# Pairing the last key tiles of a cross attention, with its bias as a column and its low parts stored for reuse

## The chip, the core and the metric

The kernel runs on one core of a Trainium2 chip. Its time is the device time of one launch in microseconds; three runs are given, with their median. Profile and trace come from one more execution of the same program.

The engines are named as in the profile: PE is TensorE (matmuls; PEld its weight loads), DVE is VectorE, ACT is ScalarE, POOL is GpSimd, SP is SyncE, from whose queue all DMAs of this kernel are issued. SBUF is the on-chip memory, PSUM the banks that matmuls write to.

## What is computed

The inputs are x (8 batches of 64 tokens, 512 wide) and a context of 8 x 1601 rows, 512 wide. Three blocks are added to x in turn: an attention block with a self attention and a cross attention (16 heads of size 128 in 8 groups), a small attention that keeps the six highest-scored partners of each token, and a feed-forward block with ternary weights. The change lies in the cross attention:

```python
kvx = jnp.einsum('bsi,oi->bso', cond, w_kv_x)
kx, vx = jnp.split(kvx, 2, axis=-1)
kx = _ln(kx.reshape(b, sc, g, d), kxln_w, kxln_b)
vx = vx.reshape(b, sc, g, d)
xout = _gqa(qx, kx, vx).reshape(b, s, nh * d)
```

Here cond is the context (sc = 1601 rows), _ln normalises each key over its 128 elements, multiplies by kxln_w and adds kxln_b, and _gqa is softmax(q k^T / sqrt(d)) v.

## The kernel before

The 1601 context rows of a batch are cut into 13 tiles (TT): twelve of 128 rows and a last one of 65. The eight key groups are worked on in two halves of four (HG = 4), so that the work is a list of 16 items: for each half, the eight batches. Each item has 13 tiles, which makes 208 steps of the main loop, numbered g; 20 more drain it. fp32 accuracy is kept by splitting an operand into a high part, rounded to the fp32r type, and a low part, the rest; a product is then three matmuls (high x high, high x low, low x high).

In each step of the main loop, by lines of the profile:

- **keys(tt)**, L529 to L553: SP loads a tile of the turned context (cTr, L533). ACT rounds it to cThi (L536), POOL subtracts to get cTlo (L537). Twelve matmuls (L542), three products over four blocks of 128 inputs, make the keys of four groups at once, 512 columns, in a PSUM bank. ACT squares them (sq, L547) and copies them (kn, L548). DVE sums the squares (kxv, L549), POOL adds EPS (L550) and takes the power -0.5 (rqk, L173), DVE multiplies (kn, L552). The mean is taken out beforehand, in the weights.
- **keys_t(tt)**, a step later, L555 to L568: four transposes (L219) bring the keys into columns. ACT multiplies by the norm's weight and adds its bias (kthi, L565); DVE makes the rest (kf, L567); ACT adds the bias to that as well (ktlo, L568). Two tiles, at the end of an item three, fill one chunk; an item has six chunks (CHUNKS).
- **scores(ci)**, L570 to L592: matmuls of queries with a chunk's keys (L587); a DVE operation copies the scores from PSUM to S and keeps their maximum (cmx, L591). In the last chunk 321 columns are filled up to 322 with a zero (L575 to L577).
- **maxima**, **exps**: the maximum over the chunks, negated (L596), is the bias of the exponential on ACT (L601).
- LAG = 17 steps later, **context**, **probs_t** and **weigh** (L636 to L678): rows of the context are loaded and split (cr, chi, clo), the exponentials are transposed (L613) and split (phi, plo), and twelve matmuls add probabilities x context to four PSUM banks (L676 to L678). In the first half the context's low part is stored to DRAM (clod<-clo, L658), in the second it is loaded from there (L655, by the helper at L130).
- **values**, **cat**: at the end of an item the sums are multiplied by the value weights.

All other work, the projections of x, self attention, the output projections, the small attention and the preparation of the ternary weights, stands in generators that are pumped a few steps in each round of the main loop (L1225 to L1229): PACE gives the number per round, its second value from round LATER = 142 on. The feed-forward block comes at the end.

Buffers come from pools with fixed numbers: three raw (shared by cTr, cr and other loads), two cThi, two cTlo, three kn, two kf. The kernel is built with a scheduler that puts each engine's instructions in order by priority, following the order of the program and the hints high_priority and issue_after; on the chip each engine and SP's queue then run strictly in that order, waiting for semaphores.

Of the kernel before, what the change touches and what calls it, by code (L numbers as in the profile page):

```python
# [11 lines left out]
F32 = mybir.dt.float32  # L12
F32R = mybir.dt.float32r
# [24 lines left out]
NCH = len(CHUNKS)  # L38
CHUNK_OF = {tt: ci for ci, ch in enumerate(CHUNKS) for tt in ch}
LAG = 17  # L40
ALL = 10 ** 6
# [1 line left out]
SPLIT = 1  # L43
FFN_AT = 6
FAR = 3
PACE = 1.55, 4
LATER = 142
TERNARY_PACE, TERNARY_AT = 0.4, 8
HELD = "held"

# [7 lines left out]
def tile_perceiver(ctx: ExitStack, tc: tile.TileContext, t: dict):  # L58
    nc = tc.nc
    V, A, GP, PE = nc.vector, nc.scalar, nc.gpsimd, nc.tensor  # L60
# [68 lines left out]
    def load(dst, src):  # L129
        nc.sync.dma_start(dst, src)  # L130
        return dst
# [4 lines left out]
    def v3(ap, g):  # L136
        return ap.rearrange("p (g k) -> p g k", g=g)
# [4 lines left out]
    class Late:  # L142
# [13 lines left out]
        ps = staticmethod(lambda tag="b": kxp())  # L156
# [79 lines left out]
    o = 0  # L236
# [24 lines left out]
    def dtile(shape, dt, tag):  # L261
        return dram.tile(shape, dt, tag=tag, name=tag)
# [7 lines left out]
    simd = [dtile([P, S], F32, f"simd{j}") for j in range(NJ - 1)]  # L270

    wpd = [dtile([P, 2, H], F32, f"wpd{c}") for c in range(32)]
    clod = [dtile([SC, H], F32, f"clod{b}") for b in range(NB)]

    codd = [dtile([3, H], F32, f"codd{b}") for b in range(NB)]
# [215 lines left out]
    def key_weights(half):  # L491
# [10 lines left out]
            (V if half else GP).tensor_tensor(lo[:, ic, :], raw, hi[:, ic, :].bitcast(F32), ALU.subtract)  # L502
        return hi, lo

    paced = [None]
    pin = [None]

    class Cross:


        def __init__(self, b, half):
            self.b, self.half = b, half
            self.raw = None
            self.S = {}
            self.kt = {}
            self.kn = {}
            self.pp = {}
# [11 lines left out]
        def keys(self, tt):  # L529

            t0, n = TT[tt]
            raw = mp.tile([P, NIC, P], F32, tag="raw", name=nm("cTr"), bufs=3)
            paced[0] = nc.sync.dma_start(raw[:, :, :n], t["ctxT"][self.b].rearrange("(c p) k -> p c k", p=P)[:, :, t0:t0 + n])  # L533
            chi = mp.tile([P, NIC, P], F32R, tag="cThi", name=nm("cThi"), bufs=2)
            clo = mp.tile([P, NIC, P], F32R, tag="cTlo", name=nm("cTlo"), bufs=2)
            A.copy(chi[:, :, :n], raw[:, :, :n])  # L536
            GP.tensor_tensor(clo[:, :, :n], raw[:, :, :n], chi[:, :, :n].bitcast(F32), ALU.subtract)  # L537
            ps = kxp()
            k = 0
            for st, mv in ((chi, self.wk[0]), (chi, self.wk[1]), (clo, self.wk[0])):  # L540
                for ic in range(NIC):
                    PE.matmul(ps[:n], lhsT=st[:, ic, :n], rhs=mv[:, ic, :], start=k == 0, stop=k == 11)  # L542
                    k += 1
            kn = mp.tile([P, 512], F32, tag="kn", name=nm("kn"), bufs=3)
            sq = mp.tile([P, 512], F32, tag="sq", name=nm("sq"), bufs=1)
            v = sm("kxv", HG)
            A.activation(sq[:n], ps[:n], AF.Square, scale=1.0 / math.sqrt(D))  # L547
            A.copy(kn[:n], ps[:n])  # L548
            V.tensor_reduce(v[:n], v3(sq[:n], HG), AX.X, ALU.add)  # L549
            GP.tensor_scalar(v[:n], v[:n], EPS, None, ALU.add)  # L550
            r = rsqrt(v[:n], n, HG, "rqk")
            pin[0] = V.tensor_tensor(v3(kn[:n], HG), v3(kn[:n], HG), r.unsqueeze(2).to_broadcast([n, HG, D]), ALU.mult)  # L552
            self.kn[tt] = kn  # L553

        def keys_t(self, tt):  # L555

            t0, n = TT[tt]
            ci = CHUNK_OF[tt]
            c0 = TT[CHUNKS[ci][0]][0]
            if ci not in self.kt:  # L560
                self.kt[ci] = [mp.tile([P, HG, KTW], F32R, tag="kt" + x, name=nm("kt" + x), bufs=2) for x in ("hi", "lo")]
            hi, lo = self.kt[ci]
            pt = transpose4(self.kn.pop(tt), n, kxp())
            o = slice(t0 - c0, t0 - c0 + n)
            A.activation(hi[:, :, o], v3(pt, HG)[:, :, :n], AF.Identity, bias=hb["kx"], scale=hw["kx"])  # L565
            kf = mp.tile([P, HG, P], F32, tag="kf", name=nm("kf"), bufs=2)
            V.scalar_tensor_tensor(kf[:, :, :n], v3(pt, HG)[:, :, :n], hw["kx"], hi[:, :, o].bitcast(F32), ALU.mult, ALU.subtract)  # L567
            A.activation(lo[:, :, o], kf[:, :, :n], AF.Identity, bias=hb["kx"])  # L568

        def scores(self, ci):  # L570
            chunk = CHUNKS[ci]
            cw = sum(TT[tt][1] for tt in chunk)
            hi, lo = self.kt.pop(ci)
            N = cw + (cw & 1)
            if N > cw:  # L575
                GP.memset(hi[:, :, cw:N].bitcast(F32), 0.0)
                GP.memset(lo[:, :, cw:N].bitcast(F32), 0.0)  # L577
            sc = mp.tile([P, HG, KTW], F32, tag="S", name=nm("S"), bufs=7)
            self.S[ci] = sc
            per = 512 // N  # L580
            for g0 in range(0, HG, per):
                bank = mainp("s")
                gs = range(g0, g0 + per)

                for k, (a, x) in enumerate(((self.qhi, hi), (self.qlo, hi), (self.qhi, lo))):
                    for i, g in enumerate(gs):
                        PE.matmul(bank[:, i * N:(i + 1) * N], lhsT=a[:, g * P:(g + 1) * P], rhs=x[:, g, :N],  # L587
                                  start=k == 0 and i == 0, stop=k == 2, skip_group_check=True)
                for i, g in enumerate(gs):
                    ps = bank[:, i * N:(i + 1) * N]  # L590
                    V.tensor_tensor_reduce(sc[:, g, :cw], ps[:, :cw], zeros.to_broadcast([P, cw]), 1.0, -3.0e38,  # L591
                                           ALU.add, ALU.max, self.mx[:, g * NCH + ci:g * NCH + ci + 1])  # L592

        def maxima(self):
            self.nmx = sm("cnm", HG)
            V.tensor_reduce(self.nmx, v3(self.mx, HG), AX.X, ALU.max, negate=True)  # L596

        def exps(self, ci, g0=0, g1=HG):
            cw = sum(TT[tt][1] for tt in CHUNKS[ci])
# [367 lines left out]
            xs.append((xr, j * P, i * P, P))  # L967
        return z, xs

    def gp_copy(dst, src):  # L970
        GP.tensor_scalar(dst, src, 1.0, 1.0, ALU.mult, ALU.mult)  # L971

    WIDEN = gp_copy, A.copy

    def ffn_weights(f, kind):
# [151 lines left out]
            token_norm(j)  # L1127
            yield

    NT = len(TT)  # L1130
    work = [Cross(b, half) for half in range(2) for b in range(NB)]
    NA = NT * len(work)
    rest = range(1, NJ)
# [3 lines left out]
    bgB = Stream()  # L1137
# [4 lines left out]
    for g in range(NA + LAG + 3):  # L1142
# [26 lines left out]
            work[nA].keys(kA)  # L1169
        if g == 0:  # L1170
            bgA.pump(ALL)
        if g == 2:
            bgA.add(norms(rest), projection("qx", range(4), rest), projection("qx", range(4, 8), range(NJ)),
                    projection("q", range(8), range(NJ)), projection("k", range(4), range(NJ)), projection("v", range(4), range(NJ)))
            bgA.add(*[self_attn(j) for j in range(NJ)])
            bgA.add(attn_consts())
# [132 lines left out]
```

## Time and profile before

| | us |
|---|---|
| median of three runs | 2000.94 |
| lowest, highest | 1998.29, 2001.81 |
| profiled execution | 1998.47 |
| its span, first to last instruction | 1996.7 |
| ACT busy | 1345.9 |
| POOL busy | 682.7 |
| mean granted TensorE clock, of full | 0.987 |

The groups that the change touches, from the page's list of the costliest (line, engine, operation, written and read tiles, shapes, count, then busy us and mean ns of one, then the idle time of its engine before it and what ended it):

```profile
L537 POOL TENSOR_TENSOR cTlo<-cTr,cThi 128x512 fp32r<-128x512 f32 (+1 forms) x208 | 271.1, 1303 | 840.7 <-PE kx L542 443.8
L549 DVE TENSOR_REDUCE kxv<-sq 128x4 f32<-128x512 f32 (+1 forms) x208 | 141.9, 682 | 228.0 <-ACT sq L547 227.7
L567 DVE SCALAR_TENSOR_TENSOR kf<-kx,cols,kthi 128x512 f32<-128x512 f32 (+1 forms) x208 | 151.1, 726 | 60.0 <-ACT kthi L565 58.8
L568 ACT ACTIVATE ktlo<-kf,cols 128x512 fp32r<-128x512 f32 (+1 forms) x208 | 147.4, 709 | 29.0 <-DVE kf L567 28.5
```

Idle time of an engine that isn't the bound costs nothing. In the lines of slices each digit is a fortieth of the span, in tenths of busy time, and 9 is 90% or more. The durations of matmuls overlap: what a matmul takes of PE is read from start to start.

### The profile page before, as it was taken

Reading aid. Unit: us, or ns where it says so; the run is one execution under the profiler, and the core shown is the slowest. Engines: PE = TensorE matmul, PEld = TensorE weight load, DVE = VectorE, ACT = ScalarE, POOL = GpSimd, SP = SyncE. Lnnn points to the kernel's source line nnn. Section 1 sums busy time; section 2 is a strip of 40 time slices with the busy share of each in tenths; the row PEclk is TensorE's granted clock in tenths of the full one; section 3 lists DMA queues with packets and bytes.
Section 4 is the critical chain, followed back from the end, with each engine's and each line's share of the span. In section 5 each row is a group of like instructions: output and inputs, shape, how many; then the busy total and the mean of one; then the engine's idle time right before and its main releaser. Section 6 shows DMA issues by size and latency. Waiting matters only on the chain. (4 is left out here: it accounts for less than half of the span.)

```text
span 1996.7 us, 32526 instructions
## 1 busy us (share of the span) xinstructions
PE 1931.5 (97%) x10709; PEld 1594.1 (80%) x10709; DVE 1357.9 (68%) x3324; ACT 1345.9 (67%) x2932; POOL 682.7 (34%) x807
## 2 busy tenths in 40 slices
PE   6899999999999999999999999999999999999998
PEld 5688887888888888888888888888877777886776
DVE  6868678667778677766775765666577665665665
ACT  6777777677778667765765655665786676676554
POOL 5443434333334434323233323323333323320132
PEclk9999999999999999999999999999999999999989
DMA  6354445466455654556886667656744633564415
GB/s 195 112 151 148 148 146 153 132 193 213 152 150 172 194 179 140 173 180 224 282 268 192 214 225 264 203 185 214 258 133 154 212 110 97 165 205 139 149 56 172
DMA packets 296507, 352.05 MB, mean 176 GB/s; under 512 B 30337, under 2 KB 191233, under 8 KB 296337
## 3 DMA queue, kind: packets, MB, share of 16 engines
q1 hardware_dynamic: 296336, 349.97, 55.8%
q8 instruction: 84, 1.38, 0.3%
q14 instruction: 87, 0.70, 0.1%
HBM read 283.94 MB, written 65.68 MB: 175 GB/s over the span
## 5 line engine op out<-in xcount | busy, mean ns | idle before, releaser
L537 POOL TENSOR_TENSOR cTlo<-cTr,cThi 128x512 fp32r<-128x512 f32 (+1 forms) x208 | 271.1, 1303 | 840.7 <-PE kx L542 443.8
L677 PE MATMUL acc<-plo,chi 128*128 128x512 f32 x768 | 311.7, 406 | 1.0 <-DVE plo L624 1.0
L678 PE MATMUL acc<-phi,clo 128*128 128x512 f32 x768 | 303.4, 396 | 0.0
L549 DVE TENSOR_REDUCE kxv<-sq 128x4 f32<-128x512 f32 (+1 forms) x208 | 141.9, 682 | 228.0 <-ACT sq L547 227.7
L542 PE MATMUL kx<-wkhi,cThi 128*128 128x512 f32 (+1 forms) x832 | 244.3, 415 | 6.6 <-DVE cmx L591 2.5
L676 PE MATMUL acc<-phi,chi 128*128 128x512 f32 x768 | 237.8, 403 | 4.6 <-ACT chi L653 3.4
L565 ACT ACTIVATE kthi<-kx,cols 128x512 fp32r<-128x512 f32 (+1 forms) x208 | 159.5, 767 | 106.8 <-PE kx L219 105.1
L542 PE MATMUL kx<-wklo,cThi 128*128 128x512 f32 (+1 forms) x832 | 231.0, 398 | 0.0
L542 PE MATMUL kx<-wkhi,cTlo 128*128 128x512 f32 (+1 forms) x832 | 226.3, 393 | 0.0
L173 POOL TENSOR_TENSOR rqk<-kxv,mhalf 128x4 f32<-128x4 f32 (+1 forms) x208 | 219.9, 1057 | 16.6
L653 ACT CAST chi<-cr 128x512 fp32r<-128x512 f32 x192 | 118.9, 619 | 137.7 <-PE acc L677 126.2
L536 ACT CAST cThi<-cTr 128x512 fp32r<-128x512 f32 (+1 forms) x208 | 125.6, 605 | 120.0 <-PE kx L542 48.4
L601 ACT ACTIVATE S<-S,cnm 128x256 f32<-128x256 f32 (+1 forms) x384 | 196.8, 520 | 1.5 <-DVE cnm L596 1.5
L567 DVE SCALAR_TENSOR_TENSOR kf<-kx,cols,kthi 128x512 f32<-128x512 f32 (+1 forms) x208 | 151.1, 726 | 60.0 <-ACT kthi L565 58.8
L542 PEld LDWEIGHTS kx<-wklo,cThi 128*128 128x128 f32 (+1 forms) x832 | 156.2, 188 | 39.7
L542 PEld LDWEIGHTS kx<-wkhi,cTlo 128*128 128x128 f32 (+1 forms) x832 | 153.5, 185 | 39.3 <-issue 0.8
L552 DVE TENSOR_TENSOR kn<-kn,rqk 128x512 f32<-128x512 f32 (+1 forms) x208 | 144.7, 695 | 57.0 <-POOL rqk L173 55.5
L542 PEld LDWEIGHTS kx<-wkhi,cThi 128*128 128x128 f32 (+1 forms) x832 | 147.2, 189 | 40.8 <-DVE cmx L591 5.0
L591 DVE CUSTOM_DVE_ANT_0 S<-s,zeros 128x256 f32<-128x256 f32 (+1 forms) x384 | 149.7, 429 | 43.8 <-PE s L587 43.5
L568 ACT ACTIVATE ktlo<-kf,cols 128x512 fp32r<-128x512 f32 (+1 forms) x208 | 147.4, 709 | 29.0 <-DVE kf L567 28.5
L676 PEld LDWEIGHTS acc<-phi,chi 128*128 128x128 f32 x768 | 139.0, 189 | 34.9 <-ACT chi L653 4.6
L677 PEld LDWEIGHTS acc<-plo,chi 128*128 128x128 f32 x768 | 145.2, 189 | 25.7 <-DVE plo L624 1.5
(339 smaller groups left out, 3938.3 us busy)
## 6 DMA issues: line engine op xcount, KB each, us to landing
cTr<-in_ctxT SPq DMA_DIRECT2D x192, 256.0 KB
cr<-in_ctx SPq DMA_DIRECT2D x192, 256.0 KB
ws<-wpd SPq DMA_DIRECT2D x88, 512.0 KB
clod<-clo SPq DMA_DIRECT2D x96, 256.0 KB
clo<-clod SPq DMA_DIRECT2D x96, 256.0 KB
wv<-in_wkv SPq DMA_DIRECT2D x64, 256.0 KB
tern<-in_ffn_w SPq DMA_DIRECT2D x64, 256.0 KB
wpd<-ws SPq DMA_DIRECT2D x32, 512.0 KB
```

Source lines behind the costliest of these rows:

```text
L173: GP.tensor_tensor(y[:n], v, mhalf[:n, :k], ALU.pow)
L537: GP.tensor_tensor(clo[:, :, :n], raw[:, :, :n], chi[:, :, :n].bitcast(F32), ALU.subtract)
L542: PE.matmul(ps[:n], lhsT=st[:, ic, :n], rhs=mv[:, ic, :], start=k == 0, stop=k == 11)
L552: pin[0] = V.tensor_tensor(v3(kn[:n], HG), v3(kn[:n], HG), r.unsqueeze(2).to_broadcast([n, HG, D]), ALU.mult)
L565: A.activation(hi[:, :, o], v3(pt, HG)[:, :, :n], AF.Identity, bias=hb["kx"], scale=hw["kx"])
L567: V.scalar_tensor_tensor(kf[:, :, :n], v3(pt, HG)[:, :, :n], hw["kx"], hi[:, :, o].bitcast(F32), ALU.mult, ALU.subtract)
L568: A.activation(lo[:, :, o], kf[:, :, :n], AF.Identity, bias=hb["kx"])
L591: V.tensor_tensor_reduce(sc[:, g, :cw], ps[:, :cw], zeros.to_broadcast([P, cw]), 1.0, -3.0e38, ALU.add, ALU.max, self.mx[:, g * NCH + ci:g ...
L601: A.activation(self.S[ci][:, g, :cw], self.S[ci][:, g, :cw], AF.Exp, bias=self.nmx[:, g:g + 1], accum_out=self.su[:, g * NCH + ci:g * NCH ...
L676: PE.matmul(self.U[ic], lhsT=chi[:n, s], rhs=phi[:n], start=tt == 0, stop=False)
L677: PE.matmul(self.U[ic], lhsT=chi[:n, s], rhs=plo[:n], start=False, stop=False)
L678: PE.matmul(self.U[ic], lhsT=clo[:n, s], rhs=phi[:n], start=False, stop=False)
```

## The change

- **Pairing.** In 14 of the 16 items (all but batches 0 and 1 of the first half) the last tile holds 64 rows of each of two neighbouring batches, 128 in all; its keys are computed once, in the even batch's round, and the odd batch's round computes none. The 65th row of all eight batches is computed in odd_keys, once per half (rounds 30 and 110), and copied to its place by ACT.
- **Bias as a column.** The norm's bias is no longer added to the keys. It gives each row of scores one and the same addend, q times bias, which the softmax takes out again. It stands as column 322 of the last chunk; its score is copied from PSUM (cqb) and enters the maximum. So L568 goes, and the operation of L567 writes ktlo itself.
- **The norm's constant** is column 129 of the squares (ksq), written once; L550 goes.
- **The turned context's low parts** of the twelve full tiles are stored to DRAM in the first half (clotd) and loaded in the second in place of L537.
- PACE and LATER change, background steps are scheduled at a lower priority, and the scratch for dynamic DMA is cut to 1024 bytes.

```diff
+UNPAIRED = 2
+ODD_AT = 30, 110
-PACE = 1.55, 4
-LATER = 142
+PACE = 1.64, 4
+LATER = 140
...
+    def normed_keys(wk, chi, clo, n, held=False):
+        ps = kxp()
+        k = 0
+        for st, mv in ((chi, wk[0]), (chi, wk[1]), (clo, wk[0])):
+            for ic in range(NIC):
+                PE.matmul(ps[:n], lhsT=st[:, ic, :n], rhs=mv[:, ic, :], start=k == 0, stop=k == 11)
+                k += 1
+        kn = mp.tile([P, 512], F32, tag="kn2" if held else "kn", name=nm("kn"), bufs=1 if held else 3)
+        sq = ksq
+        v = sm("kxv", HG)
+        A.activation(sq[:n, :, :D], v3(ps[:n], HG), AF.Square, scale=1.0 / math.sqrt(D))
+        A.copy(kn[:n], ps[:n])
+        V.tensor_reduce(v[:n], sq[:n], AX.X, ALU.add)
+        r = rsqrt(v[:n], n, HG, "rqk")
+        pin[0] = V.tensor_tensor(v3(kn[:n], HG), v3(kn[:n], HG), r.unsqueeze(2).to_broadcast([n, HG, D]), ALU.mult)
+        return kn
+    def turned(kn, n, parts, r0=0):
+        hi, lo = parts
+        pt = kxp()
+        for g in range(HG):
+            PE.transpose(pt[:, g * P:g * P + n], kn[:, g * P:(g + 1) * P], ident[r0:r0 + n, r0:r0 + n])
+        src = v3(pt, HG)[:, :, :n]
+        A.activation(hi, src, AF.Copy, scale=hw["kx"])
+        V.scalar_tensor_tensor(lo, src, hw["kx"], hi.bitcast(F32), ALU.mult, ALU.subtract)
+    def odd_keys(half):
...
+        kn = normed_keys(wk[half], chi, clo, NB)
...
+        turned(kn[:NB], NB, [x[:, :, :, 0] for x in oddk[half]])
...
+    GP.memset(ksq[:, :, D:], EPS)
...
         def keys(self, tt):
             t0, n = TT[tt]
+            pair = tt == NT - 1 and self.paired
+            if pair and self.b % 2:
+                return
...
+            for bi in range(2 if pair else 1):
+                w = S if pair else n
+                paced[0] = nc.sync.dma_start(raw[:, :, bi * S:bi * S + w], t["ctxT"][self.b + bi].rearrange("(c p) k -> p c k", p=P)[:, :, t0:t0 + w])
...
             A.copy(chi[:, :, :n], raw[:, :, :n])
-            GP.tensor_tensor(clo[:, :, :n], raw[:, :, :n], chi[:, :, :n].bitcast(F32), ALU.subtract)
...
-            GP.tensor_scalar(v[:n], v[:n], EPS, None, ALU.add)
...
+            if self.half and tt < NT - 1:
+                load(clo.bitcast(F32), clotd[self.b][tt])
+            else:
+                GP.tensor_tensor(clo[:, :, :n], raw[:, :, :n], chi[:, :, :n].bitcast(F32), ALU.subtract)
+                if tt < NT - 1:
+                    nc.sync.dma_start(clotd[self.b][tt], clo.bitcast(F32))
+            self.kn[tt] = normed_keys(self.wk, chi, clo, n, pair)
...
         def keys_t(self, tt):
...
-            A.activation(hi[:, :, o], v3(pt, HG)[:, :, :n], AF.Identity, bias=hb["kx"], scale=hw["kx"])
-            kf = mp.tile([P, HG, P], F32, tag="kf", name=nm("kf"), bufs=2)
-            V.scalar_tensor_tensor(kf[:, :, :n], v3(pt, HG)[:, :, :n], hw["kx"], hi[:, :, o].bitcast(F32), ALU.mult, ALU.subtract)
-            A.activation(lo[:, :, o], kf[:, :, :n], AF.Identity, bias=hb["kx"])
...
+            r = self.b % 2 * S
+            turned(kn[r:r + S], S, [x[:, :, o:o + S] for x in self.kt[ci]], r)
+            for x, y in zip(self.kt[ci], oddk[self.half]):
+                A.copy(x[:, :, o + S:o + S + 2], y[:, :, self.b, :])
...
         def scores(self, ci):
...
+                    if N > cw:
+                        V.tensor_copy(self.qb[:, g:g + 1], ps[:, cw:N])
         def maxima(self):
+            top = sm("ctop", HG)
+            V.tensor_reduce(top, v3(self.mx, HG), AX.X, ALU.max)
+            V.tensor_tensor(top, top, self.qb, ALU.add)
             self.nmx = sm("cnm", HG)
-            V.tensor_reduce(self.nmx, v3(self.mx, HG), AX.X, ALU.max, negate=True)
+            V.tensor_tensor(self.nmx, self.qb, top, ALU.subtract)
...
+        if g in ODD_AT:
+            odd_keys(work[nA].half)
...
-            with tc.issue_after(pin[0].ins), tc.issue_after(paced[0].ins) if bg is bgB else nullcontext():
+            with tc.issue_after(pin[0].ins), tc.issue_after(paced[0].ins) if bg is bgB else nullcontext(), tc.high_priority( -100):
                 bg.pump(n)
...
-    nc = _bacc.Bacc("TRN2", target_bir_lowering=False, num_devices=1)
+    nc = _bacc.Bacc("TRN2", target_bir_lowering=False, num_devices=1, dynamic_dma_scratch_size=1024)
```

More of the change, by code (lines that the diff above doesn't have):

```diff
@@ L38 @@
 NCH = len(CHUNKS)
+NT = len(TT)
+ODD_AT = 30, 110
+UNPAIRED = 2
 CHUNK_OF = {tt: ci for ci, ch in enumerate(CHUNKS) for tt in ch}
@@ L272, in tile_perceiver @@
     wpd = [dtile([P, 2, H], F32, f"wpd{c}") for c in range(32)]
+    clotd = [[dram.tile([P, NIC, P], F32, name=f"clotd{b}_{k}") for k in range(len(TT) - 1)] for b in range(NB)]
     clod = [dtile([SC, H], F32, f"clod{b}") for b in range(NB)]
@@ new lines, in turned @@
+    def turned(kn, n, parts, r0=0):
[6 more added lines that the diff above has]
+        V.scalar_tensor_tensor(lo, src, hw["kx"], hi.bitcast(F32), ALU.mult, ALU.subtract)
+    oddk = {}
+    def odd_keys(half):
+        raw = load(mp.tile([P, 512], F32, tag="raw", name=nm("oc"), bufs=3)[:NB], t["ctx"][:, SC - 1, :])
+        pt = kxp()
+        for ic in range(NIC):
+            PE.transpose(pt[:, ic * NB:(ic + 1) * NB], raw[:, ic * P:(ic + 1) * P], ident[:NB, :NB])
+        chi = mp.tile([P, NIC, P], F32R, tag="cThi", name=nm("cThi"), bufs=2)
+        clo = mp.tile([P, NIC, P], F32R, tag="cTlo", name=nm("cTlo"), bufs=2)
+        src = v3(pt[:, :NIC * NB], NIC)
+        A.copy(chi[:, :, :NB], src)
+        V.tensor_tensor(clo[:, :, :NB], src, chi[:, :, :NB].bitcast(F32), ALU.subtract)
+        kn = normed_keys(wk[half], chi, clo, NB)
+        oddk[half] = [const.tile([P, HG, NB, 2], F32R, tag=f"odd{x}", name=nm("odd")) for x in ("h", "l")]
+        for x, y in zip(oddk[half], kb2):
+            gp_copy(x[:, :, :, 1], y.bitcast(F32).unsqueeze(2).to_broadcast([P, HG, NB]))
+        turned(kn[:NB], NB, [x[:, :, :, 0] for x in oddk[half]])
@@ L505, in tile_perceiver, with gp_copy @@
+    def gp_copy(dst, src):
+        GP.tensor_scalar(dst, src, 1.0, 1.0, ALU.mult, ALU.mult)
+    kb = ctile([P, HG], F32, "kb")
+    kb2 = ctile([P, HG], F32R, "kbhi"), ctile([P, HG], F32R, "kblo")
+    V.tensor_copy(kb, hb["kx"].to_broadcast([P, HG]))
+    V.tensor_copy(kb2[0], kb)
+    V.tensor_tensor(kb2[1], kb, kb2[0].bitcast(F32), ALU.subtract)
+    ksq = ctile([P, HG, D + 1], F32, "ksq")
+    GP.memset(ksq[:, :, D:], EPS)
     paced = [None]
@@ L513, in __init__ @@
             self.raw = None
+            self.paired = half > 0 or b >= UNPAIRED
             self.S = {}
@@ L516, in __init__ @@
             self.kn = {}
+            self.qb = sm("cqb", HG, bufs=2)
             self.pp = {}
@@ L531, in keys @@
             t0, n = TT[tt]
+            pair = tt == NT - 1 and self.paired
+            if pair and self.b % 2:
+                return
             raw = mp.tile([P, NIC, P], F32, tag="raw", name=nm("cTr"), bufs=3)
-            paced[0] = nc.sync.dma_start(raw[:, :, :n], t["ctxT"][self.b].rearrange("(c p) k -> p c k", p=P)[:, :, t0:t0 + n])
+            if pair:
+                n = P
+            for bi in range(2 if pair else 1):
+                w = S if pair else n
+                paced[0] = nc.sync.dma_start(raw[:, :, bi * S:bi * S + w], t["ctxT"][self.b + bi].rearrange("(c p) k -> p c k", p=P)[:, :, t0:t0 + w])
             chi = mp.tile([P, NIC, P], F32R, tag="cThi", name=nm("cThi"), bufs=2)
@@ L536, in keys @@
             A.copy(chi[:, :, :n], raw[:, :, :n])
-            GP.tensor_tensor(clo[:, :, :n], raw[:, :, :n], chi[:, :, :n].bitcast(F32), ALU.subtract)
[L538 to L549, printed above, removed]
-            GP.tensor_scalar(v[:n], v[:n], EPS, None, ALU.add)
-            r = rsqrt(v[:n], n, HG, "rqk")
-            pin[0] = V.tensor_tensor(v3(kn[:n], HG), v3(kn[:n], HG), r.unsqueeze(2).to_broadcast([n, HG, D]), ALU.mult)
-            self.kn[tt] = kn
+            if self.half and tt < NT - 1:
[5 more added lines that the diff above has]
+            self.kn[tt] = normed_keys(self.wk, chi, clo, n, pair)
+            if pair:
+                work[self.half * NB + self.b + 1].kn[tt] = self.kn[tt]
         def keys_t(self, tt):
@@ L561, in keys_t @@
                 self.kt[ci] = [mp.tile([P, HG, KTW], F32R, tag="kt" + x, name=nm("kt" + x), bufs=2) for x in ("hi", "lo")]
-            hi, lo = self.kt[ci]
-            pt = transpose4(self.kn.pop(tt), n, kxp())
-            o = slice(t0 - c0, t0 - c0 + n)
-            A.activation(hi[:, :, o], v3(pt, HG)[:, :, :n], AF.Identity, bias=hb["kx"], scale=hw["kx"])
-            kf = mp.tile([P, HG, P], F32, tag="kf", name=nm("kf"), bufs=2)
-            V.scalar_tensor_tensor(kf[:, :, :n], v3(pt, HG)[:, :, :n], hw["kx"], hi[:, :, o].bitcast(F32), ALU.mult, ALU.subtract)
-            A.activation(lo[:, :, o], kf[:, :, :n], AF.Identity, bias=hb["kx"])
+            o = t0 - c0
+            kn = self.kn.pop(tt)
+            if tt < NT - 1 or not self.paired:
+                turned(kn[:n], n, [x[:, :, o:o + n] for x in self.kt[ci]])
+                if n & 1:
+                    for x, y in zip(self.kt[ci], kb2):
+                        gp_copy(x[:, :, o + n:o + n + 1], y.bitcast(F32).unsqueeze(2))
+                return
+            r = self.b % 2 * S
+            turned(kn[r:r + S], S, [x[:, :, o:o + S] for x in self.kt[ci]], r)
+            for x, y in zip(self.kt[ci], oddk[self.half]):
+                A.copy(x[:, :, o + S:o + S + 2], y[:, :, self.b, :])
         def scores(self, ci):
@@ L574, in scores @@
             N = cw + (cw & 1)
-            if N > cw:
-                GP.memset(hi[:, :, cw:N].bitcast(F32), 0.0)
-                GP.memset(lo[:, :, cw:N].bitcast(F32), 0.0)
             sc = mp.tile([P, HG, KTW], F32, tag="S", name=nm("S"), bufs=7)
@@ L968, in ffn_rows @@
         return z, xs
-    def gp_copy(dst, src):
-        GP.tensor_scalar(dst, src, 1.0, 1.0, ALU.mult, ALU.mult)
     WIDEN = gp_copy, A.copy
@@ L1128, in norms @@
             yield
-    NT = len(TT)
     work = [Cross(b, half) for half in range(2) for b in range(NB)]
```

## The prediction

> **What bounds the kernel now.** I read the page's busy table first, then the slices, then the waits of PE, then the timeline of PE for the price of one tile.
>
> ```profile
> PE 1931.5 (97%) x10709; PEld 1594.1 (80%) x10709; DVE 1357.9 (68%) x3324; ACT 1345.9 (67%) x2932; POOL 682.7 (34%) x807
> PE   6899999999999999999999999999999999999998
> PEclk9999999999999999999999999999999999999989
> DMA  6354445466455654556886667656744633564415
> ```
>
> PE is busy for 97% of the span and in the highest tenth in all but a few slices at both ends; the next engines, DVE and ACT, stand at 68% and 67%. The granted clock is full in nearly every slice, so the span is PE's work plus its gaps. A busy PE need not be dense, as the ends of matmuls are modelled, so the second view is what PE waits for from 100 to 1800 us (engine, line, releaser: total, times, longest):
>
> ```profile
> PE xo L697 <- DMA wv<-in_wkv: 4.1, 4, 1.3
> PE pt L613 <- DVE cmx L591: 3.9, 5, 1.4
> PE acc L676 <- ACT chi L653: 3.4, 2, 2.8
> PE pt L613 <- ACT S L601: 2.8, 2, 2.6
> PE kx L542 <- DVE cmx L591: 2.5, 6, 0.6
> PE pp L431 <- DMA ws<-wpd: 2.5, 3, 1.3
> ```
>
> These are the six largest; all rows of that view add up to 24 us in 1700. No other engine or queue holds PE up in the middle. What is left is at the ends: in the first 100 us PE is busy 75.8, in the last 147 us 133.0. So a change is worth what it takes from PE's instruction stream, as long as it opens no new wait. The timeline gives the price of a key tile there (start, duration, operation; a group's end overlaps the next, so starts are what counts):
>
> ```profile
> 1213.51 1.08 PE L542 MATMUL kx<-wkhi,cThi 128*128 128x512 f32 x4
> 1214.44 1.07 PE L542 MATMUL kx<-wklo,cThi 128*128 128x512 f32 x4
> 1215.34 1.07 PE L542 MATMUL kx<-wkhi,cTlo 128*128 128x512 f32 x4
> 1216.25 0.85 PE L676 MATMUL acc<-phi,chi 128*128 128x512 f32 x3
> ...
> 1222.16 1.17 PE L542 MATMUL kx<-wkhi,cThi 128*65 128x512 f32 x4
> 1223.18 1.10 PE L542 MATMUL kx<-wklo,cThi 128*65 128x512 f32 x4
> 1224.12 1.10 PE L542 MATMUL kx<-wkhi,cTlo 128*65 128x512 f32 x4
> 1225.05 0.63 PE L431 MATMUL pp<-ws,cats 128*128 128x512 f32 x2
> ```
>
> A full tile takes 1216.25 - 1213.51 = 2.74 us, the last tile with its 65 rows 1225.05 - 1222.16 = 2.89 us. Half the keys cost the whole price.
>
> **Pairing, on PE.** Of the 16 last tiles, the 14 that aren't batches 0 and 1 of the first half are computed two at a time: 7 tiles of twelve matmuls vanish. Take 2.8 us, between the two rows: 7 x 2.8 = 19.6 us. The key that is left over in each batch is computed by odd_keys, once per half: twelve matmuls with 8 stationary columns but 512 moving ones, so 2.8 us again, and 8 small transposes. The nearest row for those is four transposes of a 65-row tile, from 1791.78 to 1792.03 in the same timeline, 0.25 us; two such groups are 0.5. Twice 3.3 us is 6.6 us. The built order of the changed kernel agrees: 84 matmuls of L542 less, 24 with 8 columns and 16 small transposes more; the transposes of keys keep their number (64 columns instead of 65), the scores their width (322, where the bias column takes the place of the zero). Net on PE: 19.6 - 6.6 = **13 us less**.
>
> Here the Trainium skill speaks against the size. "TensorE: Matmul & The Clock Gate", section Back-to-back issue gap, says that a stream of weight loads and matmuls with 512 columns sustains about 131 ns each. That would make a tile 1.6 us and the net 7 x 1.6 - 2 x (1.6 + 0.5) = 7.0 us. The rows say 2.74 / 12 = 228 ns, and I take the rows; 7 us is kept as the small end.
>
> **ACT.** The second activation of each key tile goes (L568: 208 at 709 ns by its row, 147 us); the bias is no longer added, and DVE's subtraction writes the low part straight to its place. 14 pairs of small copies come, a few us. ACT falls to about 1200 us of work. It isn't the bound, so the worth on the path is near nothing, except that the chain from PE's transposed keys to the scores is shorter by 0.7 us.
>
> **DVE.** The subtraction L567 keeps its form (746 ns). New: 64 copies of one column from PSUM (a read of the accumulator takes 83 ns in the L591 group, a 128x4 operation 222 ns at L364; I take 0.15 us, 10 us in all), 32 small operations in the maxima, a sum over 129 instead of 128 columns (under 1% of 142 us), some in odd_keys. About +18 us on an engine with 640 us to spare. The copies hold a score bank a little longer, in 16 of the 96 chunks; below 0.2 us each behind a three-buffer pool, I count 0, at most 64 x 0.2 = 13 us, and no gain.
>
> **POOL and the norm's constant.** The addition at L550 (208 at about 0.26 us) goes, because EPS stands as column 129 of the squares. This shortens the chain from squares to normed keys by 0.26 us and takes 55 us off POOL. The subtraction that makes cTlo (L537) goes for the 96 full tiles of the second half: 96 x 1.35 = 130 us. POOL was at 34%; cover is complete, worth 0.
>
> **Low parts by DRAM.** 96 stores of 256 KB in the first half, 96 loads in the second, all from SP's queue. SP spends about 0.33 us on each issue: 63 us of SP. Each store waits for POOL's cTlo, and behind it in SP's order stand the next cTr, cr and weight loads; each load waits for the matmuls that free the buffer two tiles ago. PE alone waits for the loaded tile. Two things bound the cost. The kernel already does the same with clo:
>
> ```profile
> clod<-clo SPq DMA_DIRECT2D x96, 256.0 KB
> clo<-clod SPq DMA_DIRECT2D x96, 256.0 KB
> ```
>
> Same size, queue, store and load, and in no row of PE's waits does a load of clo appear. By that row the cost is 0. The rule of the skill that speaks against is in "DMA: Bandwidth & Descriptors", Latency and other measured facts: access to HBM takes 0.2 us on average but 2 us at high load. The POOL operation took 1.35; were a load 2 us later than it and on the path, 96 x 2 = 190 us would be lost. That needs the load to be on the path: key tiles start on average (1782.6 - 11.5) / 207 = 8.6 us apart (first and last start of L542), and with two cTlo buffers the load may start when the tile before last is through PE, so up to some 15 us ahead. SP's single waits in the trace are mostly below 8 us. I take 0. Bandwidth: 50 MB on top of 352 MB with a DMA share of 55.8%, so about 8 points more; the worst slices go from 0.8 to about 0.9. From 1000 to 1250 us the share was 0.71, and PE was busy 248.4 of 250 us there, so PE doesn't feel a loaded DMA. Lower bound nothing, upper bound the rival below.
>
> **Pace, priority, scratch.** Background steps are pumped faster (1.64 for 1.55, the fast pace from 140 for 142) and scheduled at lower priority: the same instructions in another order, costing nothing where PE finds something else to do. In the built order, by PE work counted at the pitches above, the last projection comes some 20 us earlier, and behind the last weighted tile the same 81 us of work remain, so the tail doesn't move. Distances between a matmul and its dependent transposes or scores are as before (median 10.5 us of PE work for normed keys, 6.9 for scores). Unknown either way: I allow 8 us of gain or loss. The smaller scratch serves a queue that moves nothing in section 3 of the page: 0.
>
> **Sum.** The profiled execution took 1998.47 us (span 1996.7); 1998.5 - 13 = 1985.5. The median of the runs shown is 2000.94, 2.5 above; from it 1988. The shorter chains may take one us more out of the 24 of waits. Forecast **1987 us**, its own range 1982 to 1993. What is late next: still PE.
>
> **Rivals.**
> 1. *The gaps shrink too* (0.18). ACT loses 11% of its work, POOL a quarter, and both chains that feed PE are shorter. Of the 24 us of PE's waits about 17.6 are on ACT and DVE; with half of them gone it is 1987 - 9 = 1978. For: ACT and DVE are named in them. Against: they are scattered, 0.6 us at a time, often on DVE, which gets more to do.
> 2. *The new order gives the gain back* (0.13). Lower priority for background work lets PE run dry where main work isn't ready, above all in the first 100 us, where PE already idles 24: the stores put SP's loads behind POOL there, and before the change PE stood 5.0 us at L340 for weights from a late load. Three such stands cost 15 us: 1987 + 15 = about 2000, within 0.2%. This also covers a smaller saving (the 131 ns) beside a few us of loss. Against: the order looks much the same.
> 3. *The loads of cTlo come late in the second half* (0.14), the one on the other side. Place: the last four of a tile's twelve matmuls, from tile 104 on, about 104 x 8.6 = 890 us. PE has no other source for them, and a wait there stops everything behind. Break-even is 13 / 96 = 0.14 us per load, or a quarter of them late by 0.55 us. If a quarter are late by 1 us, it is 24 us: 1987 + 24 = 2011. For: one queue in order, 192 more issues in it. Against: clo.
> The change not doing what it says can be left out: the built order has the 7 tiles less.
>
> **Chances.** Forecast 0.55, rivals 0.18, 0.13, 0.14. A measurement of this kernel tells about 0.2%, 4 us, from no change; that is 1997 to 2005. Faster: forecast and rival 1, with a little of rival 2: 0.75. Same 0.12, slower 0.13. Range 1975 to 2003: it takes in rivals 1 and 2 and leaves most of rival 3 out.
>
> **What would show it.** Right: PE's busy time falls by 60 long matmuls at the modelled 0.4 us less 16 short ones at 0.23, some 20 us, more than the span does; the matmuls of L542 with 65 stationary columns fall from 192 to 24; no wait of PE names cTlo; ACT falls to about 1200, POOL to about 500; PE stays at 97%. Wrong: PE rows that wait for DMA cTlo<-clotd; more idle time in the first 100 us; the first-half SP queue waiting for POOL so long that cTr comes late; or a tile of 12 matmuls with another pitch.

## The result, and the profile after

| | us |
|---|---|
| changed kernel, median of six runs | 2014.95 (2012.43 to 2016.94) |
| kernel before, on the same chip | 2001.01 (1995.88 to 2001.81) |
| ratio, with its 95% interval | 1.007 [1.0055, 1.0084] |
| span of the profiled execution, before and after | 1996.7, 2015.2 |

The change is 14 us slower, where the forecast was about 14 us faster. The busy table and the slices after:

```profile
PE 1922.7 (95%) x10665; PEld 1589.8 (79%) x10665; DVE 1350.2 (67%) x3417; ACT 1207.7 (60%) x2739; POOL 486.6 (24%) x468
...
PE   7789999999999999999999999999999999999997
...
PEclk9889999999999999999999999999999999999989
DMA  7365555667565675669687777867846744664425
```

The work went where the forecast sent it: ACT near 1200, POOL near 500, PE 44 instructions less. PE's busy time fell by 8.8 us, but the span grew by 18.5, so PE is idle 27 us more, at 95% and not 97%. The second and third slices show it, and the DMA row is higher in most slices. What PE waits for from 100 to 1800 us (engine, line, releaser: total, times, longest):

```profile
PE pp L435 <- DMA ws<-wpd: 11.7, 10, 3.1
PE pj L344 <- ACT ws L329: 7.8, 3, 6.2
PE acc L747 <- ACT phi L694: 3.4, 5, 1.4
PE tr L376 <- ACT fb L389: 2.5, 1, 2.5
PE xo L768 <- DMA wv<-in_wkv: 2.5, 4, 1.1
```

No row of PE's waits, here or over the whole span, names the loads of cTlo. The two rows on top are weights of the background work: ws, loaded or prepared late. Before they were 2.5 and, over the whole span, 5.0. All rows of this view add up to 45.8 us, where it was 24.

How such a stand looks is seen in the timeline around 100 us (rows of SP and of the two engines concerned, some left out):

```profile
94.57 0.40 SPq L604 DMA_DIRECT2D cTr<-in_ctxT  x1
...
100.79 1.19 SPq L391 DMA_DIRECT2D qxd<-fb  x2
...
102.03 0.60 SPq L604 DMA_DIRECT2D cTr<-in_ctxT  x1
...
102.73 0.52 SPq L391 DMA_DIRECT2D qxd<-fb  x1
...
103.34 1.12 SPq L133 DMA_DIRECT2D ld<-in_wqx  x2
...
107.36 0.91 ACT L329 ACTIVATE ws<-ld,cols 128x256 fp32r<-128x256 f32 x2 [1.29 <-DMA ld<-in_wqx]
...
107.92 0.58 PE L344 MATMUL pj<-ws,xq 128*128 128x256 f32 x1 [6.21 <-ACT ws L329]
...
108.30 1.91 PE L515 MATMUL kx<-wkhi,cThi 128*128 128x512 f32 x4
```

PE stands 6.21 us for a weight that ACT couldn't split because its load was issued at 103.34. SP had stood from 94.97 (94.57 + 0.40) to 100.79 for a store of qxd, which the kernel before has too, and everything behind it in its queue waited. So this stand shows what a late load costs; that the stores of cTlo make it is not shown by it (see e12). The last row shows the price of a stand beyond itself: four matmuls take 1.91 us instead of 1.08.

The price of pairing was read rightly. The tile of the left-over keys, whose forecast was 2.8 us:

```profile
249.67 1.08 PE L515 MATMUL kx<-wkhi,cThi 128*8 128x512 f32 x4
250.59 1.07 PE L515 MATMUL kx<-wklo,cThi 128*8 128x512 f32 x4
251.49 1.08 PE L515 MATMUL kx<-wkhi,cTlo 128*8 128x512 f32 x4
252.41 0.60 PE L376 MATMUL tr<-ident,fa 128*128 128x128 f32 x4
```

From start to start that is 2.74 us. The groups of key matmuls add up to 683.4 us of busy time, where before they had 701.6: 18.2 less.

### The profile page after: what moved, and what is told of

The parts are those of the page before. It is cut to its first block, busy times and chain, and to the rows that moved or that the text cites. A ratio compares the mean times of both kernels' runs of the same rounds, so it can differ in the third digit from the quotient of the medians.

```text
span 2015.2 us, 32512 instructions
## 1 busy us (share of the span) xinstructions
PE 1922.7 (95%) x10665; PEld 1589.8 (79%) x10665; DVE 1350.2 (67%) x3417; ACT 1207.7 (60%) x2739; POOL 486.6 (24%) x468
## 5 line engine op out<-in xcount | busy, mean ns | idle before, releaser
L522 DVE TENSOR_REDUCE kxv<-ksq 128x4 f32<-128x516 f32 (+1 forms) x203 | 139.4, 687 | 235.4 <-ACT ksq L520 235.1
L515 PE MATMUL kx<-wkhi,cThi 128*128 128x512 f32 x812 | 235.9, 412 | 7.9 <-ACT wkhi L505 2.3
L515 PE MATMUL kx<-wklo,cThi 128*128 128x512 f32 x812 | 224.8, 398 | 0.0
L515 PE MATMUL kx<-wkhi,cTlo 128*128 128x512 f32 x812 | 222.7, 394 | 0.0
L534 ACT ACTIVATE kthi<-kx,cols 128x512 fp32r<-128x512 f32 (+2 forms) x208 | 140.6, 676 | 104.4 <-PE kx L532 103.1
L535 DVE SCALAR_TENSOR_TENSOR ktlo<-kx,cols,kthi 128x512 fp32r<-128x512 f32 (+2 forms) x208 | 150.7, 725 | 70.7 <-ACT kthi L534 69.8
L515 PEld LDWEIGHTS kx<-wklo,cThi 128*128 128x128 f32 x812 | 153.9, 190 | 36.9
L515 PEld LDWEIGHTS kx<-wkhi,cTlo 128*128 128x128 f32 x812 | 152.7, 189 | 36.6 <-issue 1.6
L515 PEld LDWEIGHTS kx<-wkhi,cThi 128*128 128x128 f32 x812 | 145.1, 191 | 43.3 <-ACT wkhi L505 3.5
L749 PEld LDWEIGHTS acc<-phi,clo 128*128 128x128 f32 x768 | 144.8, 189 | 25.1 <-issue 0.8
```

The lines of the kernel that those rows point to most:

```text
L522: V.tensor_reduce(v[:n], sq[:n], AX.X, ALU.add)
L534: A.activation(hi, src, AF.Copy, scale=hw["kx"])
L535: V.scalar_tensor_tensor(lo, src, hw["kx"], hi.bitcast(F32), ALU.mult, ALU.subtract)
L749: PE.matmul(self.U[ic], lhsT=clo[:n, s], rhs=phi[:n], start=False, stop=False)
```

## The experiments

Eighteen kernels, each timed in five rounds beside the kernel before:

| run | what it is | median us | ratio to before |
|---|---|---|---|
| e1 | change without the DRAM detour | 1997.03 | 0.9985 [0.9975, 0.9996] |
| e2 | change with the old pace and priority | 2013.95 | 1.0063 [1.0038, 1.0088] |
| e3 | before + DRAM detour | 2013.67 | 1.0066 [1.0044, 1.0088] |
| e4 | before + new pace and priority | 2010.56 | 1.005 [1.0031, 1.0069] |
| e5 | pairing and columns, old pace | 2016.06 | 1.0084 [1.0066, 1.0101] |
| e6 | columns alone, old pace | 2007.62 | 1.004 [1.0026, 1.0055] |
| e7 | change, stores but no loads | 2010.85 | 1.0048 [1.0031, 1.0066] |
| e8 | change, detour issued from POOL's queue | 2024.19 | 1.0121 [1.0103, 1.0139] |
| e9 | columns alone, at the order of before | 2021.9 | 1.0097 [1.0078, 1.0116] |
| e10 | pairing and columns, at the order of before | 2059.06 | 1.028 [1.0258, 1.0302] |
| e11 | before + detour, at the order of before | 2013.43 | 1.005 [1.0032, 1.0067] |
| e12 | e1 at the order of the change | 2024.53 | 1.0109 [1.0091, 1.0127] |
| e13 | before, pace 1.56 | 1999.46 | 0.9987 [0.9977, 0.9998] |
| e14 | before, pace 1.54 | 2002.69 | 1.0006 [0.999, 1.0021] |
| e15 | change with detour, at the order of e1 | 2012.3 | 1.0041 [1.0023, 1.0059] |
| e16 | change, stores one tile later | 2014.28 | 1.0061 [1.004, 1.0082] |
| e17 | e7, same order, a quarter of the bytes | 2012.08 | 1.0053 [1.0037, 1.0069] |
| e18 | e1 without pairing | 2003.12 | 1.0005 [0.999, 1.002] |

A caution for all that follows: one profiled execution can lie some way off its kernel's median. That of e7 took 2003.69 us, with a median of 2010.85. So amounts come from medians, and profiles only say where time goes.

**The parts alone and taken out (e1 to e4).** My theory was that the detour is the cost, the rival that the new order is. e1 makes cTlo on POOL in both halves:

```diff
-            if self.half and tt < NT - 1:
-                load(clo.bitcast(F32), clotd[self.b][tt])
-            else:
-                GP.tensor_tensor(clo[:, :, :n], raw[:, :, :n], chi[:, :, :n].bitcast(F32), ALU.subtract)
-                if tt < NT - 1:
-                    nc.sync.dma_start(clotd[self.b][tt], clo.bitcast(F32))
+            GP.tensor_tensor(clo[:, :, :n], raw[:, :, :n], chi[:, :, :n].bitcast(F32), ALU.subtract)
```

> The changed kernel with the low parts of the turned context made on POOL in both halves, as before: no clotd stores, no loads. Theory Q (the stores and loads fill SP's queue, so that weight loads of background work come late and PE waits for them): the 31 us that are missing against the forecast come back for the most part, 1987 to 1995 us, and PE's waits at pj for ACT ws and at pp for DMA ws fall to what they were before (5 and 2.5 us). Theory O (the lower priority and the new pace of background steps put its loads and matmuls into a worse order): 2010 to 2015 us, the waits stay.

e2 and e4 exchange only these lines (and the priority of the pumped steps); e3 adds only the stores and loads to the kernel before:

```diff
-PACE = 1.55, 4
-LATER = 142
+PACE = 1.64, 4
+LATER = 140
```

> The changed kernel with PACE, LATER and the priority of background steps as before. Theory O: 1985 to 1995 us and the waits at pj and pp gone. Theory Q: 2008 to 2020 us, with waits of PE for background weights still above 20 us.

> The kernel before with only the stores and loads of cTlo added. Theory Q: 2020 to 2030 us. Theory O: 1998 to 2004 us, as the loads stand in no wait of PE and POOL was not the bound.

> The kernel before with only the new PACE, LATER and the lower priority of background steps. Theory O: 2020 to 2030 us. Theory Q: 1996 to 2006 us.

Without the detour the change is 17 us faster (1.0070 / 0.9985 = 1.0085), and the detour alone makes the kernel before 13 us slower: in both places it costs about the whole forecast gain or more. e1 came 2 us above the range of my theory, and its stands for ws didn't fall to those of before; e3 and e4 lie between the ranges named. And the new pace also cost 10 us in the kernel before and nothing in the change (e2), so the parts don't add up.

**Pairing, columns, stores, another queue (e5 to e8).** e5 is e1 with the old pace; e6 leaves out pairing as well. e7 makes cTlo on POOL in the second half but keeps the stores, which nobody then reads. e8 puts `nc.gpsimd.dma_start` for the stores and loads, so that SP has neither.

> The changed kernel without the stores and loads of cTlo and with PACE, LATER and priority as before: pairing and the two columns alone. Theory P (the pairing is worth its 13 us of PE's work, since PE stays the bound and no queue is added): 1985 to 1990 us. Rival (any new order of this kernel costs some 10 us of scattered waits, as the order edit alone cost the kernel before): 1995 to 2000 us.

> The kernel of e5_no_dram_old_order with no tile paired and no odd_keys: the bias and EPS columns alone. Theory P: PE's work is that of the kernel before, so 1998 to 2003 us, 13 us above e5; ACT at 67% was no bound. Rival (the shorter chains are what helps): 1988 to 1995 us, near e5.

> The changed kernel with the 96 stores of the first half, but cTlo made on POOL in the second half too, so that nothing is loaded. Theory S (the stores do the harm: they wait for POOL in SP's queue with the background loads behind them): 2008 to 2015 us, the same lag at 1000 us as the changed kernel. Theory L (the loads do it): 1996 to 2001 us.

> The changed kernel with the same 96 stores and 96 loads of cTlo issued from POOL's queue instead of SP's. Theory Q (the place in SP's queue costs, not the bytes): 1995 to 2002 us, PE's waits at pj and pp as without the DRAM detour. Rival B (the bytes cost: more traffic makes every load land later): 2010 to 2018 us.

The stores alone bring 12.6 of the 17 us (1.0048 - 0.9985), the loads 4.4, which the intervals don't tell from nothing. So not the loads, which PE could wait for, are the larger part, but the stores, which nobody waits for. With POOL's queue it is 10 us worse than with SP's. But e8 moves more than the place in the queue: each issue takes POOL itself 603 ns, so that POOL is busy 606 us instead of 487, and the 50.34 MB go by a queue (software_dynamic) that moves nothing in the change and for which the change cut the scratch:

```profile
L609 POOL DMA_DIRECT2D cTlo<-clotd x96 | 57.9, 603 | 554.2 <-PE kx L515 494.2 <-PE kx L532 19.9 <-PE pt L684 17.5
L613 POOL DMA_DIRECT2D clotd<-cTlo x96 | 57.9, 603 | 26.5 <-POOL cTlo L611 26.5
```

Which of these costs the 10 us was not tested. Even the two columns, which remove 416 instructions from ACT and POOL, cost 8 us at the old pace. e5, e6 and e8 lie outside both ranges that were named for them.

**A theory that fell: the order (e9 to e14).** Each edit makes the scheduler rebuild the order of all engines. I then held that this alone costs some 10 us, whatever the edit. To test it, dependencies without waits were added at the end of the build, which hold the instructions of an engine in a recorded order; new instructions find their own place:

```diff
+    for a, b in zip(want, want[1:]):
+        tc.add_manual_dep(mine[b], mine[a].name, mybir.DependencyInfo(mybir.DependencyClass.NoSync, mybir.DependencyReason.DATA), reason="order")
```

That holding adds nothing by itself is not shown by a run: the kernel before was not timed while held in its own order.

> The bias column and the constant's column alone, as in the run with the columns only (2007.6, 1.004), but every instruction that the kernel before has too is held in the order of the kernel before, on all five engines; only the copies of the bias column and the few extra maxima find their own place. It removes the 208 additions on ScalarE and on GpSimd and adds 64 short copies. My theory, that the 8.6 us of the columns came from the new order and not from the work: 1996 to 2002 (0.998 to 1.001). Rival, that the work itself costs them (the copies hold score banks, the subtraction from PSUM on VectorE holds the key's bank longer): 2005 to 2010.

> Pairing and both columns, no low parts by DRAM, the pace of before, as in the run of 2016.1 (1.0084), but TensorE, GpSimd and SyncE held in the order of the kernel before, with the 84 matmuls of the seven key tiles simply left out and the 40 of the odd keys finding their own place; ScalarE and VectorE are free. Theory of the order: the 13 us of the removed tiles show, 1985 to 1993 (0.992 to 0.996). Rival, that pairing itself stalls TensorE (a pair's two batches wait for one tile): 2005 to 2016, with waits at the paired tiles.

> The kernel before with the low parts by DRAM in it and nothing else of the change (2013.7, 1.0066 with an order of its own), now with all instructions of before held in the order of before; the 192 new transfers find their own place among SyncE's. Theory of the order: 1998 to 2004 (0.999 to 1.002). Rival, that the transfers themselves cost (SyncE stands behind GpSimd for each store, later loads come late, more traffic): 2010 to 2016.

> The changed kernel without the stores and loads of the low parts (GpSimd makes them in both halves), which had 1997.0 with an order of its own, held in the order of the changed kernel; only the 96 subtractions of the second half find their own place on GpSimd. Theory of the order: it stays at 2009 to 2015 (1.005 to 1.008). Rival, that the transfers themselves cost: 1995 to 2001.

Three of the four went against the theory, and e12 lies beyond what it named; e9 and e10 lie beyond the range of the rival too. In e9 and e11 PE runs the very sequence of before, all 10709 instructions, and the kernels are 19 and 10 us slower. An order serves only the work that it was made for: with other work in it, it costs more (e9 beside e6, e10 beside e5). e12 is to be read in that way too. What PE waits for in e12 and, below it, in e1, over the whole span:

```profile
PE pp L437 <- DMA ws<-wpd: 19.6, 13, 4.0
PE pj L346 <- ACT ws L331: 13.7, 4, 7.0
```

```profile
PE tr L222 <- DVE fa L204: 11.7, 2, 10.8
PE pj L344 <- ACT ws L329: 9.3, 4, 6.2
PE pp L435 <- DMA ws<-wpd: 7.0, 5, 3.6
```

The order of the change, without a single transfer of the detour in it, brings the late weights of the change and more: 33.3 us against 16.3 at e1's own order. The stand of 6.21 us from the timeline of the change is among them:

```profile
105.66 0.58 PE L346 MATMUL pj<-ws,xq 128*128 128x256 f32 x1 [6.28 <-ACT ws L331]
```

So these stands belong to where the order puts the loads, not to the transfers as such. It doesn't follow that any rebuilt order is bad. Two runs of before, with pace 1.56 or 1.54 instead of 1.55 and nothing else, were made to tell that:

> The kernel before with the pace of background steps 1.56 instead of 1.55, nothing else: the same instructions, in an order that moves at many places. If the orders themselves, with no work changed, are worth some 10 us: 2003 to 2015. If the order matters only by the work that is in it: 1997 to 2004, no difference.

> The same with the pace 1.54. Same expectations: orders alone 2003 to 2015 (or as far below), no difference 1997 to 2004. Together with 1.56 it says how wide the spread is that any rebuilt order brings.

Neither is slower, but only e14 is a test. In the traces, by the tiles that they work on, 7067 of PE's 10709 matmuls stand at another place in e14 than before, and only 28 in e13: it is nearly the kernel before once more, and its 0.9987 shows that 0.13% can come up with hardly a change. e14's interval ends at 1.0021, 4 us. So a rebuilt order with the same work need not cost anything, and the theory that any such order costs some 10 us is dead. That an order can cost it is shown by e4: the work of before, 5753 matmuls at another place, 10 us more.

**What of the detour costs (e15 to e17).** e15 is the complement of e12: the change with its detour, held in the order of e1.

> The changed kernel, stores and loads of the low parts in it, held in the order of the version without them (1997.0), on all engines; the 192 transfers find their place in SyncE's order. If the transfers cost by themselves, whatever the order: 2007 to 2016, as the kernel before with them at its own order (2013.4). If they cost by the order that is made around them: 1995 to 2002.

It costs 11 us there (1.0041 - 0.9985 of 2001). With e11 that is two orders made without the detour in which the transfers cost 10 to 11 us; the rest of the 13 and 17 is within the intervals, or the order made around them. The caution of e9, e10 and e12 holds here too: an order with other work in it can itself cost. Against it, the orders that the scheduler makes with the transfers in them, e3 and the change, are no faster (1.0066 and 1.0070, beside 1.0050 and 1.0041). In e16 each store is owed and issued after the next tile's load:

```diff
+            if owed:
+                ob, ot, oc = owed.pop()
+                nc.sync.dma_start(clotd[ob][ot], oc.bitcast(F32))
...
-                    nc.sync.dma_start(clotd[self.b][tt], clo.bitcast(F32))
+                    owed.append((self.b, tt, clo))
```

> The changed kernel with each store of a low part issued one tile later, after the next tile's load of keys, so that SyncE need not stand on GpSimd (183 us over 75 stands in the changed kernel). If SyncE standing behind GpSimd is what the stores cost: 2000 to 2006 and PE's waits for ws and pp fall by half. If it is the traffic or the order made around the stores: 2010 to 2018.

No gain. What SP waits for shows why, first in the change, then in e16, then in e1, which has no stores:

```profile
SPq L133 <- PE acc L749: 200.4, 81, 7.2
SPq L613 <- POOL cTlo L611: 183.0, 75, 5.6
```

```profile
SPq L133 <- PE acc L753: 198.3, 79, 7.3
SPq L605 <- POOL cTlo L615: 107.1, 50, 4.7
...
SPq L133 <- POOL cTlo L615: 41.0, 19, 3.8
...
SPq L608 <- POOL cTlo L615: 24.3, 11, 4.9
```

```profile
SPq L604 <- POOL cTlo L608: 274.3, 112, 5.2
```

The stand at the stores fell from 183 to 24 us (L608), but 148 came up at loads: the next cTr needs the buffer that POOL has still to read. In e1 SP stands 274 us for POOL without any store. All of SP's waits are 1324 us in the change and 1402 in e1. So SP standing behind POOL isn't what the stores add. e17 is e7 with the same order and the same waits on every engine; only the size differs:

```diff
-                    nc.sync.dma_start(clotd[self.b][tt], clo.bitcast(F32))
+                    nc.sync.dma_start(clotd[self.b][tt][:, :1, :], clo[:, :1, :].bitcast(F32))
```

> The version with the stores of the low parts and no loads (2010.9, 1.0048; without the stores it is 1997.0, 0.9985), held in the same order with the same waits on every engine; each of the 96 stores only moves a quarter of its bytes, 64 KB instead of 256 KB. If the bytes are what the stores cost, on the DMA engines that the loads share: 1998 to 2003. If the issue, its place in SyncE's queue or the order made around it costs: 2008 to 2013.

A quarter of the bytes, the same time (1.0053 beside 1.0048). So it isn't the 25 MB of the stores that cost either. The number of packets was not reduced with the bytes; e1, e7 and e17 in turn:

```profile
DMA packets 296535, 352.03 MB, mean 176 GB/s; under 512 B 30352, under 2 KB 191248, under 8 KB 296368
DMA packets 310361, 377.21 MB, mean 188 GB/s; under 512 B 31888, under 2 KB 192784, under 8 KB 310192
DMA packets 310361, 358.34 MB, mean 179 GB/s; under 512 B 31888, under 2 KB 205072, under 8 KB 310192
```

**What pairing is worth (e18).** e18 is e1 with `UNPAIRED = 99`, so that no tile is paired and no odd keys are left over.

> The changed kernel without pairing and without the stores and loads: the two columns and the new pace and priority are left. With pairing it took 1997.0. If pairing is worth on the path what TensorE loses in work, the forecast's 13 us, this is 2008 to 2013. If pairing brings little and the rest of the change is what moves the time: 1996 to 2003.

2003.1, at the upper end of the rival's range. Pairing is worth 4 us at the new pace (1.0005 - 0.9985), not 13. Between the two profiles PE's busy time falls by 7.6 us, not 13, and its idle time grows by 4.

## Why the prediction was wrong, point by point

From e18 to the change, the ratios give a ledger in steps of 2001 us: columns, pace and priority +1; pairing -4; stores +12.6; loads +4.4; together +14. Of the 28 us between forecast and result the detour is 17 and the pairing 9; the other 2 are the columns with the new pace, and the 1 us hoped for from shorter chains.

1. **"Low parts by DRAM ... I take 0"** is the step that failed. It was taken over from clo, whose loads appear in no wait of PE. That is true of cTlo as well, yet the detour costs 17 us in the change, 10 to 13 in the kernel before. The step asked only whether PE would wait for the loaded tile. It let 192 more issues into a queue that feeds PE's background weights and the keys, and counted 63 us of SP as free. By which way the cost reaches PE is seen only in part. PE's stands for ws by DMA or by ACT are 26.8 us in the change, 16.3 in e1, 7.5 before. That is 10.5 of the 13 us by which PE is idle longer in the change's profile than in e1's. But e12 has 33.3 without a transfer of the detour, and e15 18.3 with all of them: these stands come with the order made around the transfers. In e11, where PE keeps the sequence of before, it stands 14.0 us for weights by DMA instead of 6.6, of 13.5 us that it is idle longer:

```profile
PE xo L705 <- DMA wv<-in_wkv: 8.0, 8, 2.4
PE pp L434 <- DMA ws<-wpd: 6.0, 8, 2.0
```

In e3, idle just as long, these rows come to 6.5, no more than before. In these profiles the late keys are not the way: ACT waits for cTr, in the change and in e1,

```profile
ACT cThi L607 <- DMA cTr<-in_ctxT: 77.0, 43, 4.7
```

```profile
ACT cThi L607 <- DMA cTr<-in_ctxT: 61.4, 31, 5.4
```

where before it was 16.0 (e15, at e1's order, has 92.7); yet most of it is there in e1, which isn't slower, and PE feels one stand in each, of 1.8 us in the change and of 2.1 in e1. That of the change:

```profile
906.49 0.39 SPq L604 DMA_DIRECT2D cTr<-in_ctxT  x1
...
910.17 0.62 ACT L607 CAST cThi<-cTr 128x512 fp32r<-128x512 f32 x1 [4.07 <-DMA cTr<-in_ctxT]
...
910.84 1.87 PE L515 MATMUL kx<-wkhi,cThi 128*128 128x512 f32 x4 [1.81 <-ACT cThi L607]
```

2. **"Pairing, on PE ... 13 us less"** had the right price for each tile (2.74 us measured, 2.8 taken) and the wrong worth on the path: 4 us, with an uncertainty of about as much. PE was at 97%, but its idle time isn't fixed: it grew by 4 from e18 to e1. That PE's busy time fell by 7.6 and not by 13 is not explained. The sign that was named for it, "some 20 us", was reckoned wrongly: it adds durations that overlap, as the 18.2 of the key groups do, where PE's busy time counts an overlap once. The rule weighed against the row, 131 ns a matmul, was rightly put aside: the pitch stays at 228 ns, and 7 us would have been nearer only by chance.

3. **"POOL and the norm's constant ... worth 0", DVE "I count 0"** held only at the new pace (e18, +1). At the old one the columns cost 8 us (e6), within the bound of 13 that was named for score banks held longer. e6's profile does have two rows with that name:

```profile
PE pt L679 <- DVE cqb L654: 3.9, 3, 2.8
...
PE kx L515 <- DVE cqb L654: 2.3, 2, 1.9
```

They are 6.2 us in one execution. That this is the whole of it wasn't shown.

4. **"Pace ... I allow 8 us"** was too narrow. The new pace costs 10 in the kernel before (e4), nothing in the change (e2 against it), and gains 20 where pairing is done without the detour (e1 against e5). Pairing takes tiles, and so places for background work, away, so the pace may belong to it; that is argued, not shown, and I didn't cost the two together. Why e5 is as slow as it is stays open.

5. **The rivals.** Rival 3 named a time near the result, 2011, by a mechanism that didn't occur: no wait of PE for cTlo. Rival 2 named the place: PE's idle time in the first 200 us rose from 27.6 to 38.3, with stands at L344. But 34.5 of it is there in e1 too, without stores, so it is mostly not the stores. Rival 1, shrinking gaps, was wrong: they grew, though ACT and POOL lost what was forecast.

**What stays open** is by what a store costs. It isn't its bytes (e17), SP's stand for POOL (longer in e1, and e16 only moved it), the scheduler's own order alone (e11, e15), a reader that waits (e7), or the buffer that a store holds (in the change POOL waits for a store once, 2.7 us). What is left is that each transfer takes an issue, its packets (as many in e17 as in e7) and a place among the transfers in flight. Which of them it is was not tested: no run has the 96 issues with fewer packets behind them. The Trainium skill, "SBUF — State Buffer", section The DMA setup-cost knee, gives every transfer a fixed part of about 2 us that doesn't grow with its bytes; e17 fits it in so far as the bytes made no difference, but no run here shows the 2 us, nor that this part is what costs.

No version is clearly better than the kernel before. e1, the change without the detour, is nearest: 0.9985 [0.9975, 0.9996], a gain smaller than the 0.2% that I can tell from no change, and no larger than that of before with pace 1.56, which is nearly the same program.

## What to carry to other kernels

A transfer is not free because nobody waits for its data: here 96 stores without a reader cost 12.6 us. Measure it alone, added to the kernel before and taken out of the change, before it goes in with other edits. A piece of work removed from an engine that is 97% busy need not be worth its price: here 4 us of 13. If a scheduler orders all engines, cost a change and its pacing together, and measure a rebuilt order with no work changed before blaming the order; look in its trace whether it is another order at all.

## What was not expected of the hardware

A stand of PE can cost more than its length. After the wait of 1.81 us at 910.84, the twelve matmuls of that tile took 4.53 us from first start to the next operation at 915.37, instead of 2.74. The stretches around it in the change, with the granted clock before the two last columns:

```profile
905.00:909.00 4.00, 4.00 (x20) 2.79 (x19) 4.00 (x10) 0.62 (x1) 0.00 (x0) 1.00 0.49 135
909.00:913.00 4.00, 2.19 (x7) 1.67 (x7) 2.23 (x7) 1.24 (x2) 0.00 (x0) 0.76 0.90 295
913.00:917.00 4.00, 4.00 (x20) 3.07 (x19) 1.93 (x4) 2.15 (x5) 0.06 (x1) 0.81 0.68 177
917.00:921.00 4.00, 4.00 (x20) 3.31 (x19) 3.90 (x7) 3.36 (x8) 0.95 (x1) 1.00 0.82 260
```

The clock falls to 0.76 and 0.81 of full and is back in the next stretch: 1.8 us on top of a wait of 1.8. In the kernel before, a stand of 1.90 us that ended at 39.06 did the same (4.43 us for the next twelve), one of 1.05 that ended at 55.26 did not (2.81). Nor had I expected that 96 stores of 64 KB cost the same as 96 of 256 KB (2012.1 and 2010.9), or that the same transfers issued by POOL make the kernel 10 us slower than issued by SP.
